# A graph layer's attention row: made by transposing the features' last column and kept in PSUM, in place of a product with a repeated weight

## The chip, the cores and the metric

The kernel runs on one core of one Trainium2 chip. The metric is the device time of one execution in microseconds; the value quoted for a kernel is the median of several executions. Beside them stands one execution taken by the hardware profiler, from which all the durations come.

## The reference

32 entries of 512 nodes with 256 features pass through four layers. Layers 0 and 3 score pairs of nodes and need the score only where the adjacency matrix is not zero. Layer 1 is a residual graph convolution. Layer 2 is the one that matters here (cut, without its batch sizes):

```python
feats = jnp.einsum('bni,oi->bno', data, W1)
f1 = jnp.einsum('bno,o->bn', feats, W2) + b2[0]
logits = f1[:, :, None] + f1[:, None, :]
coefs = jax.nn.softmax(jax.nn.leaky_relu(logits) + bias1, axis=-1)
vals = jnp.einsum('bij,bjo->bio', coefs, feats)
return vals + bias2 + data
```

So each entry has a number f1 per node, and the logits need it twice: as a column (one number per row of the matrix) and as a row (the same 512 numbers on all the partitions). `bias1` is the adjacency matrix.

## The kernel before, in words

All the numbers are fp32. The adjacency matrix is sparse, so a sparse path runs (`Sparse`, `sparse_path`); a dense path stands in the program too and isn't taken with this input. The 32 entries go in eight groups of four; group 0 has the entries 0 to 3, and the entries of a group are called b0 to b3 here.

Five kinds of work exist for each group, written as generators that yield after each piece:

- `first` (L717): loads an entry, transposes it to `hT`, writes it back as `xT`, and multiplies it by the first weights (`pre`, L540), which fills a table in DRAM that the edges read.
- `edges` (L586): the sparse scores, once for layer 0 and once for layer 3. For 36 items a group, GpSimd (POOL) fetches rows of the table by an indirect DMA (L582), DVE adds (L654, 128x1024), and four DVE steps (L667, 128x256) reduce them; POOL then puts the scores into cells in DRAM by an indirect DMA (L576), from where `load` (L689) reads them back.
- `middle` (L750, `middle_one` L787): the rest of layer 0, and the layers 1 and 2, entry by entry. This is the "main" stream.
- `last` (L960, with `sums` L933): the rest of layer 3.
- the preparations of the start.

`weave` (L443) merges them by due times. The main stream's pieces have shares (`middle_shares`, L992) that spread them over a group. Where a piece of the main stream yields True, one or two pieces of the "fill" kind (`first` and `last`) are put behind it, to give TensorE work while the main stream waits. What `weave` makes is a program order; a scheduler of the framework then orders each engine's instructions, so that DVE's queue mixes edge steps, filling steps and the main stream[...]. Group 0 has no filling pieces in `middle`, and the last group's are few.

In `middle_one`, the part around the change: `yT` is completed by a DVE add (L829). Then `f1` is a product of a repeated weight vector `q_bc` with `yT` (L834), two matmuls of 128x512 that give the row on all 128 partitions at once, copied from PSUM to SBUF by ACT (L835). The weight vector is W1 times W2, computed at the start and stored as the last column of `WT_2` (L164) and repeated into `q_bc` (L165). For each of the four blocks of rows, two matmuls of 128x257 (L845) give the features and, in column 256, f1 as a column; ACT copies the features (L846); DVE adds twice the bias to the column (L849); ACT adds row and column (L851); DVE makes the leaky relu (L852), adds the adjacency and takes the smallest negated value (L854); ACT takes the exponent with its sum (L855); DVE inverts and scales (L856, L857). `put_back` (L891) transposes the block on TensorE (L896) and copies it into `eT` (L897). When all four blocks are there, `feats` times `eT` follows (L873), and the DVE step L874 ends the layer.

PSUM results of all these come from one pool of 8 buffers of one bank each (L437).

Of the kernel before, what the change touches and what calls it, by code (L numbers as in the profile page):

```python
# [8 lines left out]
F32 = mybir.dt.float32  # L9
BF16 = mybir.dt.bfloat16  # L10
I32 = mybir.dt.int32
AF = mybir.ActivationFunctionType
ALU = mybir.AluOpType
AX = mybir.AxisListType
PSUM = bass.MemoryType.PSUM

P = 128
N = 512
D = 256
NC = N // P  # L20
DC = D // P
# [18 lines left out]
def mm(nc, out, pairs):  # L40

    for n, (lhsT, rhs) in enumerate(pairs):
        nc.tensor.matmul(out, lhsT, rhs, start=(n == 0), stop=(n == len(pairs) - 1))  # L43


class Model:


    def __init__(self, ctx, tc, a):
        nc = self.nc = tc.nc  # L50
        self.tc, self.a = tc, a
        const = self.const = ctx.enter_context(tc.tile_pool(name="const", bufs=1))
        self.ident = const.tile([P, P], F32, name="ident")
        make_identity(nc, self.ident)
        self.adj = const.tile([P, NC, N], F32, name="adj")
        for c in range(NC):
            nc.sync.dma_start(self.adj[:, c, :], a["adj"][c * P : (c + 1) * P, :])
        self.g0, self.g3 = self.gnn_first("L0_gnn"), self.gnn_first("L3_gnn")
# [78 lines left out]
    def others_loads(self, raw):  # L137
        nc, a, const = self.nc, self.a, self.const
        self.b_1 = self.column("L1_gnn_b")
        self.w2 = self.column("L2_gnn_W2")  # L140
        self.b2 = self.bcast("L2_gnn_b2", 1)
        self.bias2 = self.column("L2_gnn_bias2")
        self.W1_1, self.W1_2 = raw([P, DC, D]), raw([P, DC, D])
        nc.scalar.dma_start(self.W1_1, a["L1_gnn_W"].rearrange("(c p) d -> p c d", p=P))
        nc.scalar.dma_start(self.W1_2, a["L2_gnn_W1"].rearrange("(c p) i -> p c i", p=P))
        self.twob2 = const.tile([P, 1], F32, name="twob2")
        self.WT_1 = const.tile([P, DC, D], F32, name="WT_1")
        self.WT_2 = const.tile([P, DC, D + 1], F32, name="WT_2")
        self.q_bc = const.tile([P, DC, P], F32, name="q_bc")

    def others(self, psum):
        nc = self.nc
        nc.vector.tensor_scalar(self.twob2, self.b2, 2.0, None, ALU.mult)
        for src, dst in ((self.W1_1, self.WT_1), (self.W1_2, self.WT_2)):
            for c in range(DC):
                pt = psum()
                for r in range(DC):
                    nc.tensor.transpose(pt[:, r * P : (r + 1) * P], src[:, r, c * P : (c + 1) * P], self.ident)
                nc.vector.tensor_copy(dst[:, c, 0:D], pt[:, 0:D])
            yield  # L160
        for c in range(DC):
            pq = psum()[:, 0:1]
            mm(nc, pq, [(self.W1_2[:, r, c * P : (c + 1) * P], self.w2[:, r, :]) for r in range(DC)])
            nc.vector.tensor_copy(self.WT_2[:, c, D : D + 1], pq)  # L164
            nc.vector.tensor_copy(self.q_bc[:, c, :], self.WT_2[:, c, D : D + 1].to_broadcast([P, P]))  # L165
        yield

    def adj_turned(self, c, psum):
# [246 lines left out]
class Sparse:  # L415
# [3 lines left out]
    def __init__(self, ctx, m, counts, xr, outr, B):  # L419
        self.m, self.nc, self.tc, self.counts = m, m.nc, m.tc, counts  # L420
        tc = m.tc
        self.xr, self.outr = xr, outr
        pool = lambda n, b, **k: ctx.enter_context(tc.tile_pool(name=n, bufs=b, **k))
        self.dram = pool("dram", 1, space=bass.MemoryType.DRAM)

        self.cells = {
            k: [self.dram.tile([CELLS + SPARE, NB], F32, name=f"cells_{k}{q}") for q in range(2)] for k in "03"
        }
        self.lists = self.dram.tile([N, 2 * N], F32, name="lists")
        self.x2s = self.dram.tile([B, P, NC, D], F32, name="x2s")  # L430

        self.xT, self.x2T = (self.dram.tile([B, P, DC, N], F32, name=n) for n in ("xT", "x2T"))
        self.e = Edges(m, pool("edges", 1))
        self.adjT = pool("adjT1", 1).tile([P, NC, N], F32, name="adjT")
        self.grp = pool("grp", 2)
        self.act, self.small, self.gath = pool("act", 1), pool("small", 2), pool("gath", 5)
        self.ps = pool("ps", 8, space=PSUM)  # L437
        self.later, self.bigs, self.given = None, 0, None

    def psum(self):  # L440
        return self.ps.tile([P, N], F32, name="pst", tag="pst")
# [345 lines left out]
    def middle_one(self, g0, g3, b, i, SA, keep, given):  # L787
        nc, m, w = self.nc, self.m, g0.w
        act, small, psum = self.act, self.small, self.psum
# [34 lines left out]
        yT = act.tile([P, DC, N], F32, name="yT")  # L824
# [4 lines left out]
            nc.vector.tensor_tensor(yT[:, c, :], yT[:, c, :], zT[:, c, :], ALU.add)  # L829
            yield c == DC - 1  # L830

        f1 = small.tile([P, N], F32, name="f1", bufs=1)
        pf = psum()
        mm(nc, pf, [(m.q_bc[:, c, :], yT[:, c, :]) for c in range(DC)])  # L834
        nc.scalar.copy(f1, pf)  # L835
        feats = act.tile([P, NC, D], F32, name="feats", tag="mhT0")
        eT = act.tile([P, NC, N], F32, name="eT")
        if more:
            keep[1] = turned()
            ahead = None if given else self.hWa(g0, keep[1], 0)  # L840
        yield
        exs = []
        for ic in range(NC):
            pn = psum()
            mm(nc, pn[:, 0 : D + 1], [(yT[:, r, ic * P : (ic + 1) * P], m.WT_2[:, r, :]) for r in range(DC)])  # L845
            nc.scalar.copy(feats[:, ic, :], pn[:, 0:D])  # L846
            cols = small.tile([P, 4], F32, name="cols", bufs=4)
            fcol, mn, total, rs = (cols[:, k : k + 1] for k in range(4))
            nc.vector.tensor_scalar(fcol, pn[:, D : D + 1], m.twob2, None, ALU.add)  # L849
            ex = small.tile([P, N], F32, name="ex", bufs=4)  # L850
            nc.scalar.activation(ex, f1, AF.Identity, bias=fcol)  # L851
            nc.vector.scalar_tensor_tensor(ex, ex, 0.01, ex, ALU.mult, ALU.max)  # L852

            nc.vector.tensor_tensor_reduce(ex, ex, m.adj[:, ic, :], -1.0, 3.0e38, ALU.add, ALU.min, mn)  # L854
            nc.scalar.activation(ex, ex, AF.Exp, bias=mn, scale=-1.0, accum_out=total)  # L855
            nc.vector.reciprocal(rs, total)  # L856
            nc.vector.tensor_scalar(ex, ex, rs, None, ALU.mult)  # L857
            exs.append(ex)
            yield True
            if ic > 1:  # L860
                self.put_back(eT, ic - 2, exs[ic - 2])
                yield True
# [129 lines left out]
def middle_shares(given):  # L992


    hWa = [] if given else [1.7, 1.7]
    shares = list(hWa)
    for b in range(NB):
        more = hWa if b < NB - 1 else []
        shares += [] if given else [2.8, 2.8]
        shares += [3.4, 3.4, 1.0, 2.7]  # L1000
        shares += [1.7, 3.4, 2.8, 4.5, 1.7]
        shares += [0.4, 0.4, 0.4, 1.0, 0.4, 1.0] + more + [1.5, 1.5]
        shares += [2.8, 4.5] + [0.4] * NC + [0.5, 0.5]
    return shares + [0.1]
# [46 lines left out]
def dense_path(ctx, m, xr, outr, B):  # L1051

    nc, tc, a = m.nc, m.tc, m.a
    keep = ctx.enter_context(tc.tile_pool(name="keep", bufs=1))
    act = ctx.enter_context(tc.tile_pool(name="dact", bufs=1))
    hidp = ctx.enter_context(tc.tile_pool(name="hid", bufs=4))
    small = ctx.enter_context(tc.tile_pool(name="dsmall", bufs=2))
    ps_s = ctx.enter_context(tc.tile_pool(name="ps_s", bufs=2, space=PSUM))
    ps = ctx.enter_context(tc.tile_pool(name="dps", bufs=5, space=PSUM))

    def psum(n=N):
        t = ps.tile([P, N], F32, name="dpst", tag="dpst")
        return t[:, 0:n]

    ones_row = keep.tile([1, P], F32, name="ones_row")
    nc.vector.memset(ones_row, 1.0)
    for _ in m.rest(keep.tile([P, 2048], F32, name="raw"), psum):
        pass
    adjT = keep.tile([P, NC, N], F32, name="adjT")
    for c in range(NC):  # L1070
        nc.scalar.copy(adjT[:, c, :], m.adj_turned(c, psum))
# [111 lines left out]
    def layer2(y):  # L1183
        yT = transposed(y, "dyT")
        f1 = act.tile([P, N], F32, name="df1")
        pf = psum()
        mm(nc, pf, [(m.q_bc[:, c, :], yT[:, c, :]) for c in range(DC)])
        nc.scalar.copy(f1, pf)
        feats = act.tile([P, NC, D + 1], F32, name="dfeats")
        fcol = act.tile([P, NC, 1], F32, name="dfcol")  # L1190
        yb = act.tile([P, NC, D], F32, name="dyb")
        nc.gpsimd.memset(feats[:, :, D : D + 1], 1.0)
        for c in range(NC):
            pn = psum(D + 1)
# [5 lines left out]
        for ic in range(NC):  # L1200
# [9 lines left out]
            ex = small.tile([P, N], F32, name="dex")  # L1210
# [9 lines left out]
            rs = small.tile([P, 1], F32, name="drs")  # L1220
# [61 lines left out]
```

## Time and profile before

| what | value |
|---|---|
| median of 3 executions | 3247.94 us (3246.24 to 3251.05) |
| the profiled execution | 3230.9 us |
| its span, first to last instruction | 3229.2 us |
| mean granted TensorE clock | 0.928 |
| L43, the product with `q_bc` | 128 records, 62.3 us busy |
| L835, the copy of f1 | 32, 18.8 us busy |
| L849, the column's bias | 128, 26.7 us busy |
| L896, the transposes of `ex` | 512, 88.5 us busy, 99.2 us idle before them |

A matmul in fp32 shows as two records of TensorE (PE), and a transpose as one. Ends of matmuls are modelled, so the time that one takes is best read from its start to the next start. DVE steps overlap a little at their ends as well: their mean durations add up to some 5 to 7% more than the time that a run of them takes. "PEclk" is the share of the clock that was granted. In the lists a bracket such as `[1.05 <-DVE ex L857]` says that the engine stood idle for 1.05 us and which instruction released it.

### The profile page before, as it was taken

To read this page: it belongs to the slowest core of one execution; us is meant where nothing else is said; L and a number is where in the kernel's file an instruction comes from. 1 tells how busy PE (TensorE), PEld (TensorE's weight loads), DVE (VectorE), ACT (ScalarE), POOL (GpSimd) and SP (SyncE) were. 2 spreads that over 40 slices of the span, in tenths; PEclk is the share of its full clock that TensorE was granted. 3 is DMA by queue.
4 is the path that set the end of the run, shared out by engine and by line. 5 is a ranking of instruction groups with operands and counts; after the bars stand their busy time and mean duration, and the time that the engine had idled before them with its cause. 6 is when DMAs were issued, how large, how long until landed. Compare 5 with 4: busy or idle time off the path is not lost.

```text
span 3229.2 us, 32451 instructions
## 1 busy us (share of the span) xinstructions
PE 2773.2 (86%) x8646; PEld 1656.2 (51%) x8646; DVE 2371.6 (73%) x7692; ACT 1007.0 (31%) x2341; POOL 1488.3 (46%) x1248
## 2 busy tenths in 40 slices
PE   6346887989997999979999899979998899999947
PEld 3223444546554566435654565536654465545626
DVE  7777736989596976969598786969688695953662
ACT  4452333322233222333223232333223222232441
POOL 1565402747264543636354462636355362630371
PEclk9677898999999999989999999989999999999969
DMA  8876425777567766776577766776577765640663
GB/s 273 295 246 229 152 91 166 261 262 224 188 226 240 234 196 202 249 241 220 173 230 235 245 203 211 237 250 207 178 219 246 242 221 190 219 159 33 209 201 112
DMA packets 302718, 679.40 MB, mean 210 GB/s; under 512 B 52672, under 2 KB 170944, under 8 KB 294336
## 3 DMA queue, kind: packets, MB, share of 16 engines
q0 software_dynamic: 111168, 338.90, 32.8%
q1 hardware_dynamic: 186224, 334.68, 31.0%
q10 hardware_dynamic: 5136, 3.68, 0.4%
q8 instruction: 71, 1.16, 0.1%
q14 instruction: 119, 0.97, 0.1%
HBM read 531.12 MB, written 146.01 MB: 210 GB/s over the span
## 4 chain that ended last, share of the span: by engine, by line
PE 38%; DVE 34%; DMA 17%; issue 6%; ACT 3%; POOL 1%; SPq 0%; ACTq 0%; POOLq 0%; DVEq 0%
PE pst L43 28%; DVE rows L667 11%; DVE rows L654 10%; DMA rows<-table,iv 6%; DMA table<-puv 4%; PE pst L945 4%; PE pst L802 2%; DMA cells<-s,cell 2%; PE pst L954 1%; DVE ex L852 1%; PE pst L896 1%; DMA cells<-self_s 1%; PE pst L809 1%; DVE ex L854 1%; DMA mine<-table,iu 1%
## 5 line engine op out<-in xcount | busy, mean ns | idle before, releaser
L582 POOL DMA_INDIRECT rows<-table,iv x554 | 680.1, 1228 | 1047.4 <-DMA table<-puv 383.1
L576 POOL DMA_INDIRECT cells<-s,cell x576 | 684.3, 1188 | 592.7 <-DMA cells<-s,cell 357.0
L654 DVE TENSOR_TENSOR rows<-rows,mine 128x1024 f32<-128x1024 f32 x554 | 667.3, 1215 | 195.0 <-DMA rows<-table,iv 178.9
L667 DVE SCALAR_TENSOR_TENSOR rows<-rows,L_gnn_W2bc 128x256 f32<-128x256 f32 x2016 | 750.9, 413 | 0.4
L43 PE MATMUL pst<-adj,h 128*128 128x512 f32 x1024 | 453.5, 592 | 0.0
L43 PE MATMUL pst<-L_gnn_Wa,hT 128*128 128x256 f32 x1024 | 260.6, 408 | 142.4 <-DMA hT<-xT 69.4
L43 PE MATMUL pst<-w_L_gnn_W,hT 128*128 128x512 f32 x512 | 261.2, 646 | 57.4 <-ACT hT L537 46.3
L43 PEld LDWEIGHTS pst<-adj,h 128*128 128x128 f32 x1024 | 192.8, 190 | 219.5 <-issue 214.1
L43 PEld LDWEIGHTS pst<-L_gnn_Wa,hT 128*128 128x128 f32 x1024 | 207.8, 208 | 187.8 <-issue 103.2
L43 PE MATMUL pst<-w_L_gnn_W,yT 128*128 128x512 f32 x512 | 239.9, 622 | 66.0 <-DVE yT L874 66.0
L43 PE MATMUL pst<-eT,feats 128*128 128x512 f32 x512 | 240.0, 624 | 9.1 <-ACT eT L897 9.1
L43 PE MATMUL pst<-adjT,zW 128*128 128x512 f32 x512 | 225.9, 592 | 0.0
L550 ACT COPY puv<-pst 128x256 f32<-128x256 f32 x256 | 94.7, 372 | 412.5 <-DVE puv L549 376.2
L945 PEld LDWEIGHTS pst<-hWa,SA 128*128 128x128 f32 x896 | 213.4, 328 | 5.9 <-issue 3.3
L945 PE MATMUL pst<-hWa,SA 128*128 128x256 f32 x896 | 216.2, 397 | 0.0
L43 PEld LDWEIGHTS pst<-w_L_gnn_W,yT 128*128 128x128 f32 x512 | 101.8, 200 | 196.3 <-issue 111.0
L549 DVE TENSOR_TENSOR puv<-pst,bc_L_gnn_b 128x256 f32<-128x256 f32 x256 | 106.6, 417 | 127.4 <-PE pst L43 64.4
L771 ACT COPY flat<-SA 128x512 f32<-128x512 f32 x128 | 134.5, 1122 | 203.3 <-PE pst L43 178.8
L802 PE MATMUL pst<-flat,hWa 128*128 128x512 f32 x448 | 196.8, 592 | 0.0
L43 PEld LDWEIGHTS pst<-w_L_gnn_W,hT 128*128 128x128 f32 x512 | 102.0, 206 | 168.0 <-issue 90.5
L43 PE MATMUL pst<-WT,hT 128*128 128x256 f32 x512 | 141.8, 434 | 38.8 <-DVE hT L810 38.8
L896 PE MATMUL pst<-ident,ex 128*128 128x128 f32 x512 | 88.5, 302 | 99.2 <-DVE ex L857 62.6
(167 smaller groups left out, 3728.0 us busy)
## 6 DMA issues: line engine op xcount, KB each, us to landing
table<-puv SPq DMA_DIRECT2D x256, 256.0 KB, 4.9
SA<-cells SPq DMA_DIRECT2D x64, 1024.0 KB, 7.0
h<-in_x_dram SPq DMA_DIRECT2D x64, 512.0 KB, 6.6
mine<-table SPq DMA_DIRECT2D x64, 512.0 KB, 6.2
hT<-xT SPq DMA_DIRECT2D x36, 512.0 KB, 5.0
h<-x2s SPq DMA_DIRECT2D x36, 512.0 KB, 6.1
xT<-hT SPq DMA_DIRECT2D x32, 512.0 KB, 7.5
x2T<-yT SPq DMA_DIRECT2D x32, 512.0 KB, 5.0
```

The source lines that it names most:

```text
L43: nc.tensor.matmul(out, lhsT, rhs, start=(n == 0), stop=(n == len(pairs) - 1))
L549: nc.vector.tensor_tensor(puv[:, 0, :], pp[:, 0:D], w["b1bc"], ALU.add)
L550: nc.scalar.copy(puv[:, 1, :], pp[:, D:])
L576: self.nc.gpsimd.indirect_dma_start(out=g.cells[half], out_offset=bass.IndirectOffsetOnAxis(ap=at, axis=0), in_=s, in_offset=None)
L582: self.nc.gpsimd.indirect_dma_start(out=rows, out_offset=None, in_=g.table, in_offset=bass.IndirectOffsetOnAxis(ap=at, axis=0))
L654: nc.vector.tensor_tensor(rows, rows, other, ALU.add)
L667: nc.vector.scalar_tensor_tensor(part, part, 0.0, w["W2bc"], ALU.max, ALU.mult, accum_out=at)
L771: self.nc.scalar.copy(flat[:, r, :], SA[r][:, :, b])
L802: nc.tensor.matmul(pz, hWa[:, r, cs], flat[:, r, :], start=(r == 0), stop=False)
L809: nc.tensor.matmul(pz, w["Wm"][:, d, cs], mhT[:, d, :], start=False, stop=(d == DC - 1))
L896: nc.tensor.transpose(pt[:, js], ex[:, js], self.m.ident)
L945: nc.tensor.matmul(pz[:, k * D : (k + 1) * D], SA[r][:, cs, b], hWa[:, r, :], start=(r + k == 0), stop=False)
```

## The change

The product with `q_bc` goes, and so does its copy to SBUF. All four blocks' features are made first, 257 columns wide, so that f1's column lies in SBUF with them. One DVE step adds twice the bias to all four columns. Four transposes on TensorE, each of a column repeated 128 times, write the row onto all the partitions of a PSUM bank, and ACT's step reads the row from there. The bank is a pool of its own; the common pool has 7 buffers. The features yield four pieces, of which the third and fourth allow filling work, and no feature matmuls stand between the softmax blocks. `q_bc` is kept for the dense path alone.

```diff
-        self.ps = pool("ps", 8, space=PSUM)
+        self.ps = pool("ps", 7, space=PSUM)
+        self.ps_f1 = pool("ps_f1", 1, space=PSUM)
...
-        f1 = small.tile([P, N], F32, name="f1", bufs=1)
-        pf = psum()
-        mm(nc, pf, [(m.q_bc[:, c, :], yT[:, c, :]) for c in range(DC)])
-        nc.scalar.copy(f1, pf)
-        feats = act.tile([P, NC, D], F32, name="feats", tag="mhT0")
+        feats = act.tile([P, NC, D + 1], F32, name="feats", tag="mhT0")
         eT = act.tile([P, NC, N], F32, name="eT")
         if more:
             keep[1] = turned()
             ahead = None if given else self.hWa(g0, keep[1], 0)
-        yield
-        exs = []
         for ic in range(NC):
             pn = psum()
             mm(nc, pn[:, 0 : D + 1], [(yT[:, r, ic * P : (ic + 1) * P], m.WT_2[:, r, :]) for r in range(DC)])
-            nc.scalar.copy(feats[:, ic, :], pn[:, 0:D])
+            nc.scalar.copy(feats[:, ic, :], pn[:, 0 : D + 1])
+            yield ic > 1
+
+        fcol = small.tile([P, NC, 1], F32, name="fcol", bufs=1)
+        nc.vector.tensor_scalar(fcol, feats[:, :, D : D + 1], m.twob2, None, ALU.add)
+        f1 = self.ps_f1.tile([P, N], F32, name="f1")
+        for ic in range(NC):
+            nc.tensor.transpose(
+                f1[:, ic * P : (ic + 1) * P], feats[:, ic, D : D + 1].to_broadcast([P, P]), m.ident
+            )
+        exs = []
+        for ic in range(NC):
             cols = small.tile([P, 4], F32, name="cols", bufs=4)
-            fcol, mn, total, rs = (cols[:, k : k + 1] for k in range(4))
-            nc.vector.tensor_scalar(fcol, pn[:, D : D + 1], m.twob2, None, ALU.add)
+            mn, total, rs = (cols[:, k : k + 1] for k in range(3))
             ex = small.tile([P, N], F32, name="ex", bufs=4)
-            nc.scalar.activation(ex, f1, AF.Identity, bias=fcol)
+            nc.scalar.activation(ex, f1, AF.Identity, bias=fcol[:, ic, :])
...
-        shares += [1.7, 3.4, 2.8, 4.5, 1.7]
+        shares += [1.7, 3.4, 2.8, 4.5] + [0.9] * NC
```

In the changed kernel the lines of the sparse path move: the features' copy is L839, the columns' bias L843, the new transposes L846, row plus column L854, and the four steps after it L855, L857, L858 and L859 with L860; the edge steps L654 and L667 are L653 and L666 there, L712, L938 and L957 are L711, L941 and L960, and L874 is L877.

More of the change, by code (lines that the diff above doesn't have):

```diff
@@ L148, in others_loads @@
         self.WT_2 = const.tile([P, DC, D + 1], F32, name="WT_2")
-        self.q_bc = const.tile([P, DC, P], F32, name="q_bc")
     def others(self, psum):
@@ L164, in others @@
             nc.vector.tensor_copy(self.WT_2[:, c, D : D + 1], pq)
-            nc.vector.tensor_copy(self.q_bc[:, c, :], self.WT_2[:, c, D : D + 1].to_broadcast([P, P]))
         yield
@@ L1063, in psum @@
         return t[:, 0:n]
+    q_bc = keep.tile([P, DC, P], F32, name="q_bc")
     ones_row = keep.tile([1, P], F32, name="ones_row")
@@ L1068, in dense_path @@
         pass
+    for c in range(DC):
+        nc.vector.tensor_copy(q_bc[:, c, :], m.WT_2[:, c, D : D + 1].to_broadcast([P, P]))
     adjT = keep.tile([P, NC, N], F32, name="adjT")
@@ L1186, in layer2 @@
         pf = psum()
-        mm(nc, pf, [(m.q_bc[:, c, :], yT[:, c, :]) for c in range(DC)])
+        mm(nc, pf, [(q_bc[:, c, :], yT[:, c, :]) for c in range(DC)])
         nc.scalar.copy(f1, pf)
```

## The prediction

> **What bounds the kernel now.** I read the page first, then the PE's waits, then a table of stretches, then the timelines of one softmax stage on PE and on DVE.
>
> ```profile
> span 3229.2 us, 32451 instructions
> ...
> PE 2773.2 (86%) x8646; PEld 1656.2 (51%) x8646; DVE 2371.6 (73%) x7692; ACT 1007.0 (31%) x2341; POOL 1488.3 (46%) x1248
> ...
> PE 38%; DVE 34%; DMA 17%; issue 6%; ACT 3%; POOL 1%; SPq 0%; ACTq 0%; POOLq 0%; DVEq 0%
> ```
>
> PE and DVE share the chain that ended last, so no single engine's busy time is the bound. The next view has a row for each stretch from the f1 product to the first product with `eT`: entries b0, b1, b2, b3 of group 2, then an entry of group 0, which has no filling work.
>
> ```profile
> core 0: us, PE busy (x) PEld busy (x) DVE busy (x) ACT busy (x) POOL busy (x), PEclk, DMA share, GB/s
> 909.90:936.10 26.20, 22.73 (x109) 19.46 (x108) 26.20 (x89) 11.42 (x25) 17.98 (x15) 1.00 0.50 152
> 995.90:1033.40 37.50, 30.36 (x101) 17.63 (x99) 25.00 (x92) 16.85 (x40) 10.16 (x10) 0.86 0.58 202
> 1101.10:1128.80 27.70, 25.10 (x117) 21.74 (x116) 27.64 (x96) 12.01 (x26) 21.00 (x18) 1.00 0.74 239
> 1188.70:1211.80 23.10, 22.63 (x92) 16.29 (x90) 12.05 (x29) 11.30 (x23) 2.72 (x3) 1.00 0.64 216
> 419.70:438.00 18.30, 9.84 (x37) 6.71 (x35) 9.23 (x25) 11.72 (x24) 0.00 (x0) 0.83 0.08 30
> ```
>
> In b0 and b2 DVE never rests; in b3 PE never does; b1 waits; in group 0 both rest and the chain of dependent steps sets the time. b2 in detail, on PE and then on DVE:
>
> ```profile
> 1101.09 1.88 PE L43 MATMUL pst<-yT,q_bc 128*128 128x512 f32 x4
> 1102.80 1.03 PE L43 MATMUL pst<-WT,yT 128*128 128x257 f32 x4
> 1103.67 7.63 PE L945 MATMUL pst<-hWa,SA 128*128 128x256 f32 x32
> ...
> 1116.33 0.60 PE L896 MATMUL pst<-ident,ex 128*128 128x128 f32 x4
> ...
> 1118.85 0.63 PE L896 MATMUL pst<-ident,ex 128*128 128x128 f32 x4 [1.05 <-DVE ex L857]
> ...
> 1128.84 0.59 PE L43 MATMUL pst<-eT,feats 128*128 128x512 f32 x1
> ```
>
> ```profile
> 1099.57 0.68 DVE L829 TENSOR_TENSOR yT<-yT,hT 128x512 f32<-128x512 f32 x1
> ...
> 1110.20 0.48 DVE L857 TENSOR_SCALAR ex<-ex,cols 128x512 f32<-128x512 f32 x1
> ```
>
> PE fills the time until the first `ex` (ready at 1110.7) with feats and with the last layer's products, and waits only 1.05 and 1.55 us for later ones.
>
> [...]four 128x128 transposes take 0.44 us to the next start (1116.33 to 1116.77), while four matmul records of 128x512, which are two matmuls, take 1.71 (1101.09 to 1102.80). [...] Here a gap of 1.95 us was enough:
>
> ```profile
> 1298.00 3.04 PE L43 MATMUL pst<-L_gnn_Wa,hT 128*128 128x256 f32 x8
> ...
> 1298.60:1302.00 3.40, 3.40 (x11) 2.72 (x11) 3.40 (x17) 2.16 (x6) 2.63 (x3) 0.50 0.70 157
> ```
>
> The same eight took 1.89 at full clock (1119.31). [...]
>
> **The change, part by part** (against the profiled execution: 3230.9 us, of which 3229.2 span; it lies 17.0 under the median of 3247.94, and I shift my sum by that).
>
> *Removed.* Two products per entry: 1.71 us of PE, 32 entries. The f1 copy on ACT (L835, 0.59) lies beside PE's feats and is worth nothing except where the chain is bare. Three of four L849 (0.13 to the next start each): 0.4 us of DVE an entry. Two setup copies of q_bc, 0.4 us once.
>
> *Added.* Four transposes: 0.44 us of PE, if a repeated column loads like `ex`. The trace has no such load; a bound above is the 328 ns weight load of L945 against 155 for L896, +0.7 an entry, below it is nothing less than 0.44. I take 0.44, so PE gains 1.27 an entry, 41 us in all. L851 reading PSUM: 685 ns (L828, from PSUM) against 718, nothing. 257 columns in feats' copy: nothing.
>
> *Moved: the softmax start.* All four feats, the whole fcol and the transposes now come before the first exponent; before, the first exponent needed one feats. Then the four chains run abreast. No DMA's work is changed; SP passes the same descriptors, with hT's read one table write earlier, and the SA load still ahead of the xT write that b1 waits for (SP issues it at 1009.21, xT at 1009.63).
>
> *Group 0 and the tail (no filling work).* Entry at 419.75: its last L829 ends 421.36. New chain: feats copied 423.8, transposes 424.1, four L854 of 0.63 to 427.0, DVE's second and third steps interleaved (eight of 0.6, with Exp of 0.9 beside), first `ex` 430.7, last 433.3, transposes and copy (at half clock) 435.2. Before, eT was complete at 438.02: gain 2.8. The old order had the last chain start only at 432.4, after its feats had waited behind a transpose; that wait disappears and next late is DVE itself. Entries 0 and 1 have DVE edge steps between: the sum of DVE work before the fourth `ex` falls from 18.9 and 19.9 to 13.4 and 13.0, gain 5 and 6. Likewise entry 4: 2.6; 29: 4; 30: 2.1; 31: 2.3; entry 28 loses 0.6. Together about -27 us.
>
> *b2 (six entries).* In the built order DVE has before the first L860: 22 L666 of 0.345, 6 L653 of 1.215, 10 steps of 128x512 at 0.68, the multiply 0.49 and 0.7 of small ones and accumulator reads; 22.9 us by rows. The old order's sum to the first L874 is 34.6 by rows and took 32.8, so I scale by 0.945: 21.6, and `ex` is ready at 1100.25 + 21.6 = 1121.9. PE wants it at 1101.1 + six feats matmuls 2.6 + filling 3.7 + 0.9 + 3.7 + transposes 0.44 + 3.6 = 1116.0. It waits 5.9. The second `ex` costs 0.75, the third 1.0, and filling 1.8 + 3.6 + 1.8 follows: the eT product starts at 1132.5 instead of 1128.8, and 0.8 later still for a part of a half-clock window: +4.5. What is queued behind: `h` and eT products, and all of PE. The old sum to the first `ex` was 11.1. This is the main loss.
>
> *b0 (five entries).* The same with 25.3 by rows times 0.934 (37.0 took 34.55): 23.65 after the L829 that ends at 905.46. PE starts feats 4.6 later and wants `ex` at 19.5: waits 4.1, 0.8, 0.8, and reaches the eT product 31.7 after 905.46 instead of 30.7: +1.0.
>
> *b3 (six).* No edges. The transposes wait for 3.6 and 3.4 us of filling work; first `ex` 5.4 us after them, PE wants it after 3.4: waits 2.0 and 0.9 less 1.27 gained, less the old 0.5: +0.4, and 0.5 us of filling goes elsewhere: +1.
>
> *b1 (six).* PE's time hangs on the xT write (7.4 us from 1009.63) and on the filling pieces after it; it gains about what lies after: -1.
>
> *Bunched edges.* In b0 and b2 DVE now asks for six edge steps in 17 to 20 us. POOL needs a fetch (1.23) and a put (1.19) for each with 0.30 between, 3.0 us; DVE asks each 2.8 to 3.2. With three fetched ahead it is nearly enough: bounds 0 and 3, I take 1.0 for eleven entries: +11.
>
> Sum: -27 + 27 + 5 + 6 - 6 + 11 = +16: 3246.9 profiled, 3264 as a median.
>
> **Rivals.**
> *A, faster.* The edge steps pulled forward (one more in b0's stretch, two in b2's, about 2.7 us each) are DVE work that later need not be done. PE waits per group for edges' ends: 1.8 and 4.6 in b1, 12.45 for yT behind the next edges' first row, 3 for zT at 1255. If the SA load is released as much earlier as the edges are, b0 and b2 are repaid: about 32 of the loss goes, without the POOL stretch too: -27, 3221. Against it: the 12.45 hangs on the new table's landing, not on old edges. It decides from 3 us per group given back.
> *B, seven banks.* PE waits for a bank that DVE holds (L960 and L711 stand behind edges). The trace has no PE wait of that kind; at 1 us an entry, +32 more: 3296.
> *C, a wash.* The PE gain of 41 and the waits cancel: 3248.
> That the product stays is excluded: the built order has no q_bc in the sparse path.
>
> **How the numbers follow.** Forecast (slower, 3255 to 3285) 0.45; A 0.25; C 0.20; B and worse 0.10. This kernel's times can tell about 0.2%, 6.5 us, from no change. Faster 0.25, same 0.20, slower 0.55. The range 3222 to 3300 leaves out part of A and of B; the likeliest case's own is 3255 to 3285.
>
> **What would show it.** Right: the idle before the `ex` transposes (99.2 us in the groups by line now) grows to about 150 while group 0's shrinks; q_bc's 62 us of PE are gone and 14 of transposes appear; the edge rows (L653) wait longer for POOL. Wrong: PE waits of under 2 us in b2, or PE waiting for evacuation steps, or L854's mean well above 0.72.

## The result, and the profile after

The changed kernel takes 3224.22 us (median of 11 executions, 3217.82 to 3237.16); the kernel before, beside it on the same chip, 3247.25 us (11 executions). The ratio is 0.9939 with a 95% interval of 0.9928 to 0.995: 0.6% faster. On a second chip it was 0.9953 (0.994 to 0.9966). The forecast was slower, 3264. The page of the changed kernel, in the lines that answer to those of before:

```profile
span 3220.7 us, 32267 instructions
...
PE 2741.7 (85%) x8645; PEld 1652.4 (51%) x8646; DVE 2351.1 (73%) x7594; ACT 980.4 (30%) x2309; POOL 1472.2 (46%) x1248
...
PE 35%; DVE 27%; DMA 12%; issue 5%; ACT 2%; POOL 1%; SPq 0%; DVEq 0%; ACTq 0%; POOLq 0%
```

PE's busy time fell by 31.5 us against the first profile, the span by 8.5 only, and the medians by 23. The first profile of before was a quick execution, or one on a quicker chip: at 3230.9 us it lies under all eleven executions timed beside the change (3238.42 to 3251.05), its chip isn't known, and three of the chips used below have medians of 3229 to 3231 for this kernel. A second profile of the same kernel (the run "again" below) has a span of 3251.9, and I compare with that one from here on. Cut at two marks in every entry, the DVE add that completes `yT` ("y") and the first product with `eT`, the two traces differ like this, in us, entries 0 to 31:

| stretch | predicted | measured, after less again |
|---|---|---|
| group 0, y to eT, four entries | -16.6 | -19.1 |
| entry 4 and the tail (28 to 31), y to eT | -10.4 | -7.0 |
| b2, y to eT, one entry (mean of groups 2 to 6) | +4.5 | +4.15 |
| b0 | +1.0 | +2.5 |
| b1 | -1 | +3.7 |
| b3 | +1 | 0.0 |
| from eT to the next y: ahead of b0, b1, b2, b3 | 0, and +1 for POOL | 0.0, -2.6, -6.3, 0.0 |
| groups 1 to 6 without entry 4's own stretch, sum | +43 | +7 |

So the gains of group 0 came, and the later `eT` products of the steady groups came too, even more of them than forecast. But what lies between the stretches grew shorter by 9 us a group, and that the forecast had not. The next two views show it for b1 and b2 of group 2: four stretches each (from eT of b0 to y of b1, from y to eT of b1, from eT of b1 to y of b2, from y to eT of b2), first of before (the run again), then of after.

```profile
core 0: us, PE busy (x) PEld busy (x) DVE busy (x) ACT busy (x) POOL busy (x), PEclk, DMA share, GB/s
948.02:1007.60 59.58, 57.99 (x156) 27.71 (x154) 55.97 (x207) 16.07 (x31) 38.90 (x34) 1.00 0.83 272
1007.60:1045.08 37.48, 29.70 (x99) 17.48 (x98) 24.93 (x91) 16.85 (x40) 10.89 (x10) 0.86 0.63 203
1045.08:1110.45 65.37, 54.44 (x145) 27.51 (x146) 47.71 (x162) 12.90 (x22) 27.92 (x22) 0.92 0.79 246
1110.45:1141.58 31.13, 27.69 (x118) 23.65 (x117) 28.80 (x98) 11.97 (x26) 21.32 (x19) 0.89 0.72 232
```

```profile
core 0: us, PE busy (x) PEld busy (x) DVE busy (x) ACT busy (x) POOL busy (x), PEclk, DMA share, GB/s
922.62:979.00 56.38, 55.76 (x152) 27.09 (x150) 54.63 (x203) 15.72 (x30) 36.29 (x31) 1.00 0.83 268
979.00:1020.95 41.95, 28.95 (x104) 17.08 (x103) 25.55 (x92) 16.49 (x40) 11.99 (x11) 0.88 0.70 235
1020.95:1081.11 60.16, 51.78 (x135) 26.12 (x136) 44.65 (x152) 12.87 (x22) 24.92 (x20) 0.91 0.75 227
1081.11:1115.51 34.40, 30.15 (x126) 24.98 (x125) 32.69 (x106) 11.38 (x25) 23.88 (x21) 0.90 0.70 226
```

The first column after the window is its length: +4.47 in b1 and +3.27 in b2, and -3.20 and -5.21 ahead of them. The PE counts tell half of the reason: ahead of b2 there are 135 matmul records where there were 145, and in b2 there are 126 where there were 118 (four of the product are gone, and four transposes are in). Filling work went over. The timelines of PE show which; before (again), then after:

```profile
1096.56 3.60 PE L43 MATMUL pst<-adj,h 128*128 128x512 f32 x8
1099.99 7.03 PE L43 MATMUL pst<-adjT,zW 128*128 128x512 f32 x16
1106.86 3.60 PE L43 MATMUL pst<-adj,h 128*128 128x512 f32 x8
1110.29 1.88 PE L43 MATMUL pst<-yT,q_bc 128*128 128x512 f32 x4
...
1130.44 0.88 PE L896 MATMUL pst<-ident,ex 128*128 128x128 f32 x3 [3.44 <-DVE ex L857]
```

```profile
1077.84 0.59 PE L43 MATMUL pst<-adjT,zW 128*128 128x512 f32 x1
1078.27 7.03 PE L43 MATMUL pst<-adj,h 128*128 128x512 f32 x16
1085.13 2.77 PE L43 MATMUL pst<-WT,yT 128*128 128x257 f32 x12
...
1096.08 0.60 PE L846 MATMUL f<-ident,feats 128*128 128x128 f32 x4
1096.51 3.62 PE L957 MATMUL pst<-L_gnn_Wm,mhT 128*128 128x256 f32 x16
1104.38 2.17 PE L899 MATMUL pst<-ident,ex 128*128 128x128 f32 x8 [4.25 <-DVE ex L860]
...
1115.51 1.02 PE L43 MATMUL pst<-eT,feats 128*128 128x512 f32 x2
```

Before, eight records of `adj,h` (filling work) stood ahead of the products that make `yT` (`adjT,zW`) and eight behind; after, all 16 stand behind, so 4.0 us of filling lie between y (at 1081.11) and the features. Averaged over the groups 2 to 6, b2's stretch holds 3.8 us more of `adj,h` and the stretch ahead of it 3.8 us less. The new transposes take 0.43 us to the next start, close to the forecast's 0.44, and the wait for the first exponential is there, 4.25 us. The groups by line, with the idle time ahead of them in the third field, again and then after:

```profile
L896 PE MATMUL pst<-ident,ex 128*128 128x128 f32 x512 | 90.3, 306 | 108.3 <-DVE ex L857 75.8 <-DVE cols L856 19.6 <-DVE s L571 5.9
L43 PE MATMUL pst<-w_L_gnn_W,yT 128*128 128x512 f32 x512 | 237.0, 616 | 72.9 <-DVE yT L874 72.9
L654 DVE TENSOR_TENSOR rows<-rows,mine 128x1024 f32<-128x1024 f32 x554 | 667.9, 1216 | 206.7 <-DMA rows<-table,iv 189.6 <-DMA mine<-table,iu 16.9
```

```profile
L899 PE MATMUL pst<-ident,ex 128*128 128x128 f32 x512 | 97.1, 329 | 105.7 <-DVE ex L860 59.5 <-DVE cols L859 45.9
L43 PE MATMUL pst<-w_L_gnn_W,yT 128*128 128x512 f32 x512 | 240.5, 623 | 44.9 <-DVE yT L877 44.9
L653 DVE TENSOR_TENSOR rows<-rows,mine 128x1024 f32<-128x1024 f32 x554 | 667.6, 1217 | 185.5 <-DMA rows<-table,iv 158.0 <-DMA mine<-table,iu 27.3
L846 PE MATMUL f<-ident,feats 128*128 128x128 f32 x128 | 21.9, 277 | 0.8
```

The waits for `ex` are not 150 us but 106, the wait for `yT` at the end of b1 fell from 73 to 45, and the edge rows wait less, not more.

For the steady groups I use one account more. A group's length is PE's idle time (the length less PE's busy time), plus the clock that was not granted while PE was busy (half of the busy time at half clock; half clock while PE idles is in the idle time already), plus the rest, which is PE's work at full clock. Means of the groups 2 to 6 from one profiled execution of each kernel; the experiments are told below:

| kernel | one group, us | PE idle | clock lost | work |
|---|---|---|---|---|
| before: first profile, again | 370.7, 372.7 | 31.4, 33.9 | 10.0, 9.5 | 329.4, 329.3 |
| after: first profile, after2 | 374.1, 374.6 | 37.0, 37.8 | 12.8, 12.4 | 324.3, 324.4 |
| ordprod | 382.2 | 37.7 | 15.0 | 329.5 |
| f1sbuf | 380.5 | 39.7 | 16.7 | 324.1 |
| shares17 | 377.6 | 40.0 | 13.2 | 324.4 |
| noprod | 369.4 | 34.9 | 11.2 | 323.3 |
| early, early2 | 366.6, 368.5 | 32.2, 32.7 | 9.3, 10.9 | 325.1, 324.9 |
| earlyprod | 368.5 | 29.4 | 9.9 | 329.2 |
| pad1 | 376.2 | 36.2 | 12.1 | 327.8 |
| pad3 | 377.4 | 35.1 | 14.3 | 328.0 |

After against again: work -4.9, idle +3.1, clock lost +3.3, so +1.5 a group. The work is about 329 us in every kernel with the product and 324 to 325 with the transposes (pad1 and pad3 add 3.4 to that), so the product's time is really saved; in the steady groups waits and half clock eat it up. From chip to chip the median of the kernel before goes from 3229 to 3252 us, which would be 2.6 us in a group. A smaller difference between rows from different chips, the +1.5 among them, is therefore not shown by this table; that the groups 1 to 7 together come out even is shown by the run steadynew.

### The profile page after: what moved, and what is told of

It is laid out like the page before. It is cut to its first block, busy times and chain, and to the rows that moved or that the text cites. A ratio compares the mean times of both kernels' runs of the same rounds, so it can differ in the third digit from the quotient of the medians.

```text
span 3220.7 us, 32267 instructions
## 1 busy us (share of the span) xinstructions
PE 2741.7 (85%) x8645; PEld 1652.4 (51%) x8646; DVE 2351.1 (73%) x7594; ACT 980.4 (30%) x2309; POOL 1472.2 (46%) x1248
## 3 DMA queue, kind: packets, MB, share of 16 engines
q0 software_dynamic: 111168, 338.90, 33.9%
## 4 chain that ended last, share of the span: by engine, by line
PE 35%; DVE 27%; DMA 12%; issue 5%; ACT 2%; POOL 1%; SPq 0%; DVEq 0%; ACTq 0%; POOLq 0%
PE pst L43 24%; DVE rows L666 9%; DVE rows L653 8%; DMA rows<-table,iv 5%; PE pst L948 4%; DMA table<-puv 3%; PE pst L801 2%; DMA cells<-s,cell 2%; PE pst L899 2%; PE pst L957 1%; DVE ex L855 1%; DMA mine<-table,iu 1%; PE pst L808 1%; DVE both L551 1%; DVE puv L548 1%
## 5 line engine op out<-in xcount | busy, mean ns | idle before, releaser
L581 POOL DMA_INDIRECT rows<-table,iv x554 | 671.2, 1212 | 1060.3 <-DMA table<-puv 392.8
L653 DVE TENSOR_TENSOR rows<-rows,mine 128x1024 f32<-128x1024 f32 x554 | 667.6, 1217 | 185.5 <-DMA rows<-table,iv 158.0
L666 DVE SCALAR_TENSOR_TENSOR rows<-rows,L_gnn_W2bc 128x256 f32<-128x256 f32 x2016 | 749.4, 416 | 0.4
L43 PE MATMUL pst<-L_gnn_Wa,hT 128*128 128x256 f32 x1024 | 274.1, 423 | 131.6 <-DMA hT<-xT 75.9
L43 PEld LDWEIGHTS pst<-L_gnn_Wa,hT 128*128 128x128 f32 x1024 | 216.5, 217 | 176.4 <-issue 104.6
L948 PE MATMUL pst<-hWa,SA 128*128 128x256 f32 x896 | 217.2, 398 | 0.0
L948 PEld LDWEIGHTS pst<-hWa,SA 128*128 128x128 f32 x896 | 213.8, 328 | 6.0 <-issue 3.3
L899 PE MATMUL pst<-ident,ex 128*128 128x128 f32 x512 | 97.1, 329 | 105.7 <-DVE ex L860 59.5
L566 ACT ACTIVATE s<-s,L_gnn_nb 128x16 f32<-128x16 f32 (+2 forms) x176 | 53.5, 304 | 411.4 <-DVE rows L666 399.6
```

The lines of the kernel that those rows point to most:

```text
L566: self.nc.scalar.activation(t, t, AF.Exp, bias=w["nb2"], scale=-1.0)
L581: self.nc.gpsimd.indirect_dma_start(out=rows, out_offset=None, in_=g.table, in_offset=bass.IndirectOffsetOnAxis(ap=at, axis=0))
L653: nc.vector.tensor_tensor(rows, rows, other, ALU.add)
L666: nc.vector.scalar_tensor_tensor(part, part, 0.0, w["W2bc"], ALU.max, ALU.mult, accum_out=at)
L899: nc.tensor.transpose(pt[:, js], ex[:, js], self.m.ident)
L948: nc.tensor.matmul(pz[:, k * D : (k + 1) * D], SA[r][:, cs, b], hWa[:, r, :], start=(r + k == 0), stop=False)
```

## The experiments

My theory on seeing the result: the new order makes group 0 and the tail shorter, and in the steady groups it costs about what the transposes save. The rivals: the saved PE time makes the gain everywhere; or it is the seven banks or the first profile that misled. All ratios are to the kernel before on the same chip. The kernels of one set ran on one chip. The sets were: again, bank7, ordprod and g0new; steadynew, shares17, noprod and early; f1sbuf, earlyprod and earlysh; pad1 and pad3; after2 and early2.

**again**: the kernel before, no edit.

> The kernel before, unchanged, profiled once more. The profiled execution of before took 3230.9 us where its executions have a median of 3247; that of after took 3222.5, at its own median of 3224. If the first profile of before was only a lucky one, this profile lies near 3247 and the 16 us between the two profiles lie in the steady groups 1 to 6, where the profile of after shows 20 us more than the first profile of before. If instead the steady groups of before take the same time here as in its first profile, the gain of 23 us is somewhere that I have not seen. The ratio of the times is 1.000.

Ratio 1.0 (0.9988 to 1.0013); span of the profile 3251.9. Up to the last entry's first product with `eT` it is 20.9 us behind the first profile, and nearly all of that lies in b2's stretches (+10.5 from y to eT, +8.2 ahead of it, six entries). So the steady groups of the first profile were the quick ones, and b2's old waits of 1.05 and 1.55 us, with which I forecast, are short: b2 waits 3.6 us as a mean here, 3.0 there.

**bank7**:

```diff
-        self.ps = pool("ps", 8, space=PSUM)
+        self.ps = pool("ps", 7, space=PSUM)
```

> The kernel before with a common PSUM pool of 7 buffers in place of 8, and nothing else. My theory (the softmax order brings the gain in group 0 and the tail, and the steady groups come out even): no change, 3247 within 6 us, because PE nowhere waits for a bank in the trace of before. The rival (seven banks cost time, and the change gains more than it shows): 1 us an entry or more, 3265 to 3280, and gaps of PE released by copies of older results.

Ratio 1.0006 (0.9996 to 1.0017). Rival B of the forecast falls: in the old order a bank less cost nothing.

**ordprod**:

```diff
         f1 = self.ps_f1.tile([P, N], F32, name="f1")
-        for ic in range(NC):
-            nc.tensor.transpose(
-                f1[:, ic * P : (ic + 1) * P], feats[:, ic, D : D + 1].to_broadcast([P, P]), m.ident
-            )
+        mm(nc, f1, [(m.q_bc[:, c, :], yT[:, c, :]) for c in range(DC)])
```

(Not shown: `q_bc` is made at the start again.)

> The changed kernel in everything but one thing: the row f1 is again the product of the repeated weight with yT (two matmuls of 128x512), written into f1's own bank at the place of the four transposes. So the order, the shares and the banks of after with the PE work of before: 1.27 us of PE an entry more than after. If the order makes the gain: group 0 and the tail keep it less 1.27 an entry (8 entries, 10 us), and in the steady groups the waits of PE for the first exponential (4.2 us in b0 and b2, 1.6 in b3) and for hT (10 in b1) take the 1.27 in: 3224 + 10 = 3234, within 5. If the PE time makes it: 32 times 1.27, 41 us, 3265.

3292.25 us, ratio 1.0132 (1.0113 to 1.0151). Both expectations fall: the same order with the product is 1.3% slower than before, and 1.8 to 1.9% slower than with the transposes, 60 us for 41 us of PE. Group 0 and the tail pay 17 us (10 expected); of the 19.1 us that group 0 gains from y to eT, this run keeps 11.2, so the order alone makes more than half of it. In the steady groups the waits did not take the 1.27 us in, for a reason that I had overlooked: the product stands ahead of the chain, so the first exponents end 0.9 to 1.3 us later, and PE's wait behind it stays (b2 4.7 us in both). With it the order alone costs 9.5 us in each steady group (382.2 against 372.7 on the same chip: idle time +3.8, clock lost +5.5), which is what I had forecast in kind; the transposes give 8.1 back, of which 5.2 are work and 2.3 clock.

**g0new**: both ways stand in the kernel, and a flag chooses; `given` is set in group 0 alone.

```diff
+        new = bool(given)
+        if not new:
...
+            mm(nc, pf, [(m.q_bc[:, c, :], yT[:, c, :]) for c in range(DC)])
...
-        shares += [1.7, 3.4, 2.8, 4.5] + [0.9] * NC
+        shares += [1.7, 3.4, 2.8, 4.5] + ([0.9] * NC if given else [1.7])
```

> The changed way in group 0 alone (features first, transposes, f1 in PSUM, its shares), the old way (product, interleaved softmax, its shares) in the groups 1 to 7; banks 7 and 1. The profiles of after and before differ by -19.7 us at the end of group 0's last softmax. If group 0 and the tail make the gain and the steady groups come out even: 3247 - 20 = 3227, within 5. If the gain is spread over all entries as PE time: 4 of 32 entries' part of 23, 3 us, 3244.

3228.75, ratio 0.9941 (0.9922 to 0.9959): 19 us. Group 0's four stretches shorten by 19.2 us, as in after. Entry 2 of group 0 after, its stretch and PE in it:

```profile
410.80:423.80 13.00, 6.52 (x30) 5.12 (x28) 7.21 (x21) 10.50 (x22) 0.00 (x0) 0.74 0.12 42
```

```profile
412.68 0.95 PE L846 MATMUL f<-ident,feats 128*128 128x128 f32 x4
419.33 3.80 PE L899 MATMUL pst<-ident,ex 128*128 128x128 f32 x16 [5.70 <-DVE cols L859]
423.81 1.55 PE L43 MATMUL pst<-eT,feats 128*128 128x512 f32 x3 [0.67 <-ACT eT L900]
```

It takes 13.0 us from y, where the forecast had 13.8 and before took 16.7: the four chains run abreast and one long wait is left.

**steadynew**: the complement.

```diff
-        new = bool(given)
+        new = not given
...
-        shares += [1.7, 3.4, 2.8, 4.5] + ([0.9] * NC if given else [1.7])
+        shares += [1.7, 3.4, 2.8, 4.5] + ([0.9] * NC if not given else [1.7])
```

> The complement of the run that changed group 0 alone: group 0 the old way, groups 1 to 7 the changed way with its shares. If the parts add up (group 0 alone gave -23 us by medians, -20 by the ratio; all together -23): -3 to -6, 3246, with the last group giving 6 and the steady groups costing 2. If group 0's new way is also what lets the later groups start well: slower than before, 3255 or more.

3239.78, ratio 1.0009 (0.9998 to 1.002). The parts add up: -0.59% and +0.09%, where both together gave -0.61% and -0.47%. Group 0 is the whole net gain: by the first table, the rest of the groups 1 to 6 loses what entry 4 and the tail gain (+7 and -7.0).

**shares17**:

```diff
-        shares += [1.7, 3.4, 2.8, 4.5] + [0.9] * NC
+        shares += [1.7, 3.4, 2.8, 4.5] + [0.425] * NC
```

> The changed kernel with the features' four pieces at 0.425 each, 1.7 together as the one piece before, instead of 3.6; so the edges' due times stand against the main stream as before. Built, b2 has 5 edge steps instead of 6 ahead of the first exponential, b0 has 6 still. Theory one (edge steps pulled forward are repaid, rival A of the prediction): no gain, 3224 within 6; b2's wait falls by 1 to 3 us and the yT wait (9.0 us in after, 12.4 before) grows by as much. If edge steps pulled forward are the loss that the prediction counted: 3 us in each b2 stay won, 3224 - 18 = 3206.

3244.95, ratio 1.0029 (1.0017 to 1.0041), 0.8 to 0.9% slower than after: neither number. A group is 3.4 us longer than in after, and b3 alone 3.6, where a filling piece moved behind three blocks' transposes (waits of 1.55, 0.41 and 1.77 us in a row, a PEclk of 0.62 from 1192.67 to 1200.62, and 5.88 us for the 16 records of L948 behind them, where after took 4.00). The other three entries cancel to 0.2: b2 3.0 shorter from y to eT and 2.2 longer ahead of it, b1 1.4 longer in all. So in this profile edge steps pulled forward are repaid, and b2's wait did not even fall (5.5).

**noprod**: the product goes from the kernel before, with its copy; a part of the adjacency matrix stands in for the row, so what comes out is not the layer's result.

```diff
-        f1 = small.tile([P, N], F32, name="f1", bufs=1)
-        pf = psum()
-        mm(nc, pf, [(m.q_bc[:, c, :], yT[:, c, :]) for c in range(DC)])
-        nc.scalar.copy(f1, pf)
+        f1 = m.adj[:, 0, :]
```

> The kernel before without the product and its copy: the row f1 is replaced by the first 128 rows of the adjacency matrix, so the logits are other numbers and the exponents need not wait for a product. 1.71 us of PE an entry fall away in the old order. Theory one (PE time counts in the steady groups: there after's order cost 8.1 us a group more with the product than with the transposes, for 5.1 us of PE): -2 to -2.7 an entry in 24 steady entries, and in group 0 and the tail the 1.71 and a copy of 0.6 on the bare chain, -18: 3250 - 48 to -65 - 18 = 3167 to 3184. Theory two (the edges' chain sets the steady groups' length, and the old order's waits take the PE time in): -18 and 1.7 in each b3, 3222.

3200.06, ratio 0.9889 (0.987 to 0.9907), 36 us for 55 us of PE: between the two. In the old order a steady group gains 3.3 us against again for the 6.8 of four products: the work falls by 6.0, and idle time takes 1.0 and the clock 1.7 of it. This split is rough, since again ran on another chip and the profiled execution was the slowest of noprod's four.

**f1sbuf**: in after, ACT copies the row to SBUF.

```diff
+        f1 = small.tile([P, N], F32, name="f1", bufs=1)
+        nc.scalar.copy(f1, pf)
```

(Not shown: `pf` is the bank that the transposes write.)

> The changed kernel with one copy more: the row of f1 is copied by ACT from its PSUM bank to SBUF, as before, and ACT's step reads it there. If keeping it in PSUM matters where the chain is bare: +0.6 to 0.9 us in each entry of group 0 and the tail (+6), and in the steady groups +0.6 in b0, b2 and b3 of which half comes back (+6): 0.4% over after, a ratio to the kernel before of 0.998. If ACT (30% busy) hides the copy: the ratio of after, 0.994.

3264.6, ratio 1.0103 (1.0086 to 1.012), far over both expectations: 1.5 to 1.7% over after, 50 us, for a copy of 0.6 us in 32 entries. A group is 6.3 longer: 2.7 of idle time and 3.9 of clock. (The built order moves with it: 7 edge steps instead of 6 stand ahead of b0's first exponential.) b3 shows how a short delay is doubled; after, then f1sbuf:

```profile
1191.32 0.66 PE L899 MATMUL pst<-ident,ex 128*128 128x128 f32 x4 [1.55 <-DVE ex L860]
1192.39 0.66 PE L899 MATMUL pst<-ident,ex 128*128 128x128 f32 x4 [0.41 <-DVE ex L860]
1192.88 4.00 PE L948 MATMUL pst<-hWa,SA 128*128 128x256 f32 x16
```

```profile
1199.33 0.66 PE L901 MATMUL pst<-ident,ex 128*128 128x128 f32 x4 [2.27 <-DVE ex L862]
1200.99 0.66 PE L901 MATMUL pst<-ident,ex 128*128 128x128 f32 x4 [1.00 <-DVE ex L862]
1201.49 5.51 PE L950 MATMUL pst<-hWa,SA 128*128 128x256 f32 x16
```

The two waits grow by 0.72 and 0.59, and then the same 16 records take 5.51 us instead of 4.00: PEclk is 0.79 in the 8 us from 1199.30, where it is 1.00 in those from 1191.30 in after. It is 0.79 behind these waits in three of the five b3 and 1.00 in two.

**early**: the filling work behind the transposes instead of ahead of them.

```diff
-            yield ic > 1
+            if ic < NC - 1:
+                yield False
...
                 f1[:, ic * P : (ic + 1) * P], feats[:, ic, D : D + 1].to_broadcast([P, P]), m.ident
             )
+        yield True
```

> The changed kernel with its filling work moved: none between the features and the transposes of f1, and the piece that yields True stands right behind the transposes. In the built order DVE then has 2 edge steps instead of 6 before the first exponential in b2 and 3 instead of 6 in b0, and PE has 10 us of filling between the transposes and the first exponential's transposes. Theory one (the order costs about 9 us of a steady group because edge steps and filling stand ahead of the chain, and the transposes' PE time pays it back): PE's waits for the first exponential (4.6 us in b0, 4.7 in b2, 2.0 in b3, means of after) fall under 1 us each, 9 us a group; half of it comes back as longer waits in b1 for hT and in b2 for yT, so -5 a group: 3224 - 30 = 3194, within 15. Theory two (the steady groups' length is set by the edges, the cells' load and hT, whatever PE does): only b3's 2 us are won, 3212, and the waits in b1 and for yT grow by 7 us a group.

3175.71, ratio 0.9825 (0.9805 to 0.9845), about 39 us under after, where the theories had 30 (within 15) and 12; beside after on one chip (**early2** with **after2**) 3171.99 against 3214.6. It beats both kernels. The stretches from y to eT of b0 and b3 in group 2 of after (b2's stands above), and those of b0, b2 and b3 here:

```profile
889.47:922.62 33.15, 28.27 (x122) 22.69 (x120) 31.19 (x102) 11.08 (x25) 21.64 (x19) 0.95 0.60 181
...
1175.25:1198.48 23.23, 21.27 (x90) 15.56 (x88) 10.42 (x27) 10.27 (x22) 2.78 (x3) 1.00 0.59 200
```

```profile
882.89:909.56 26.67, 24.51 (x116) 20.62 (x114) 26.67 (x90) 10.43 (x25) 15.76 (x13) 1.00 0.56 169
...
1076.53:1105.03 28.50, 27.20 (x125) 23.06 (x124) 28.50 (x101) 11.22 (x25) 21.14 (x18) 1.00 0.63 200
...
1164.78:1185.60 20.82, 20.82 (x90) 15.57 (x89) 10.57 (x26) 9.96 (x22) 4.50 (x4) 1.00 0.47 145
```

33.2, 34.4 and 23.2 us in after became 26.7, 28.5 and 20.8, with a PEclk of 1.00. By the means of the groups 2 to 6 the three win 15.1 us, of which the stretches ahead of b1 and b2 give back 2.2 and 7.0; a group ends 7.5 us shorter (idle -4.8, clock -3.4, work +0.7), and 6.1 shorter in early2 against after2, on one chip.

> The early order, unchanged, in one set with the changed kernel: if the ratios hold between sets, 0.9825 within 0.2% and 1.15% under the changed kernel.

> The changed kernel unchanged, beside the kernel before on one more chip, and in one set with the early order. The kernel before took 3231 to 3252 us in the sets so far, so times of different sets are compared by their ratios to it. If that is sound, the ratio is again 0.994 within 0.2%. If it moves by more (0.997 or 0.991), the prices of single edits that I have taken from ratios of different sets are uncertain by 10 us.

early2 0.9822 (0.9802 to 0.9843), after2 0.9953: ratios of different sets agree within 0.15%, 5 us.

**earlyprod**: early with the product.

```diff
-        for ic in range(NC):
-            nc.tensor.transpose(f1[:, ic * P : (ic + 1) * P], feats[:, ic, D : D + 1].to_broadcast([P, P]), m.ident)
+        mm(nc, f1, [(m.q_bc[:, c, :], yT[:, c, :]) for c in range(DC)])
         yield True
```

> The early order (features, row of f1, filling behind it) with the product of the repeated weight in place of the four transposes: 1.27 us of PE an entry more than the run with the early order. Theory one (PE's time by the records is all that the transposes save): +41 us, 1.3%, a ratio to the kernel before of 0.995; the order alone is then worth 0.5% without any transpose. Theory two (the product costs what it cost in the order of after, 66 us or 2.1 an entry, since it also lengthens waits and half-clock stretches): 1.003.

3194.92, ratio 0.9903 (0.9876 to 0.9929). The order alone, without any transpose, gains 1%; and here the transposes are worth 0.8%, 25 us by the ratios (20 by the medians beside earlysh, on one chip), less than both theories. The work differs by 4.1 us a group from early, and idle time takes 2.8 of it.

**earlysh**: early with the shares of shares17.

```diff
-        shares += [1.7, 3.4, 2.8, 4.5] + [0.9] * NC
+        shares += [1.7, 3.4, 2.8, 4.5] + [0.425] * NC
```

> The early order with the features' pieces at 0.425 each instead of 0.9, so that the edges' due times stand against the main stream as in the kernel before. In after the same edit made it 0.9% slower; its profile puts that on b3 alone (21.5 us in six entries, where a filling piece moved behind three blocks' transposes), with the other entries' gains and losses cancelling. If b3's filling was the cause: in the early order b3 has no waits to lengthen (10 us of filling stand ahead), so the same time as the early order, 0.9825 within 0.3%. If edge steps that come earlier against the main stream are a gain in themselves: 0.9% slower here too, 0.991.

3175.32, ratio 0.9827 (0.981 to 0.9844): as early. With b3's 3.6 us in shares17, this fits that b3's filling made shares17 slow, and not the edges.

**pad1** and **pad3**: eight matmuls of the features once more, in b1 or in b3.

```diff
+        if b == 1 and not given:
+            for ic in range(NC):
+                pn = psum()
+                mm(nc, pn[:, 0 : D + 1], [(yT[:, r, ic * P : (ic + 1) * P], m.WT_2[:, r, :]) for r in range(DC)])
         xT = yT
```

> The changed kernel with 3.44 us of PE work added in b1 of the groups 1 to 7: the features' eight matmuls are made a second time, right ahead of the first product with eT, into buffers that nobody reads. Theory (PE's wait for yT at the end of b1, 9.0 us, ends at a fixed time, about 147 us after the yT of b0 is complete, when the first edge row of the next set can be added; what b0 and b1 lose ahead of it is taken in there): the six steady groups pay 0 to 1 us each and the last group 3.4, together 3 to 9, a ratio to the kernel before of 0.995 to 0.997, and the wait for yT falls to about 5.6. Rival (a loss of PE time anywhere in a steady group lengthens it): 7 times 3.44, 24 us, 1.001.

> The same addition in b3 of the groups 1 to 7, where PE never rests and no wait follows until b0's hT of the next entry: both theories expect the whole 7 times 3.44, 24 us, a ratio of 1.001; if less than 15, the gates reach into b3 too.

pad1 3232.49, ratio 1.0003 (0.9986 to 1.0019); pad3 3247.34, ratio 1.0052 (1.0037 to 1.0067). On one chip the same 3.44 us cost 15 us less in b1 than in b3, 2.1 in each of seven groups. By the profiles a steady group grows by 2.0 in pad1 and by 3.3 in pad3. So the waits behind b1 do take in a part, but not nearly all, as my theory had it: the wait for `yT` fell from 9.0 to 7.5 only, and b2's wait for its first exponential rose from 4.7 to 6.2.

## Why the prediction was wrong

- **Group 0 and the tail: right.** -27 forecast, -26 measured in the stretches from y to eT (-19.1 and -7.0); g0new shows 19 us for group 0 by itself.
- **The single prices: right.** Transposes 0.44 (0.43 measured; a matmul of as many columns takes 0.86, half of the product's 1.71, so column for column the traces show a factor of two), a repeated column loads like `ex` (weight load 137 ns in the median, 142 for `ex`), the step from PSUM 687 ns (685 forecast), the features' copy 374 ns with 257 columns (370 with 256), seven banks nothing (a ratio of 1.0006 in the old order).
- **b2, "This is the main loss", +4.5 in each of six entries: the failed step.** The first exponential came 23.5 us after y (21.6 forecast) and eT 34.8 after it (32.3 forecast, and 0.8 for half clock). So the delay of eT was there, +4.15 by the mean for +4.5. The fault was to book a later eT as lost time, and to put at nothing what the stretch ahead of it would give back: that one became 6.3 us shorter, so the two together end 2.15 us earlier. From y to eT 3.8 us are filling work that the stretch ahead of y no longer has, which I had not seen in the built order: I let PE start the features 0.85 us after y, where 4.0 passed. So PE asked in group 2 for the first exponential 3.3 us later than I had it, DVE had it ready 1.6 us later (it waits 1.35 us for edge rows there), and 5.9 became 4.25; and ahead of y 3.8 us are given back. The wait for `yT` there is also 3.5 shorter. In the group's account PE's idle time grew by 3.1 us, where my waits came to 9.7 more than before (2.2 in b0, 5.1 in b2, 2.4 in b3). By stretch: b0 +1.0, b2 +1.1, b3 +1.5, b1 +3.5, mostly for hT, and -3.5 ahead of b2, for yT. A part of the rest is the first profile, whose b2 waited less (3.0 us against 3.6).
- **b0, b3, b1.** First exponential of b0 after 23.9 us (23.65 forecast), its waits 4.2, 0.4 and 0.3 in group 2 (4.1, 0.8, 0.8), b3's 1.55 and 0.41 (2.0 and 0.9): right to half a microsecond. b0's eT still came 1.5 us later than forecast; a PEclk of 0.95 in its stretch of group 2 (1.00 in again) makes 1.7. b1 was called -1 and came +3.7, with 2.6 back ahead of it.
- **Half clock: too small.** 0.8 in b2 forecast, 3.3 a group measured.
- **Bunched edges, +11: wrong.** The edge rows waited 21 us less in all than in again (9.5 less than in the first profile). From y to eT they wait in b2's stretch alone, 1.7 us, where it was 1.5 in again already.
- **Rival A had the number, 3221, and not the whole mechanism.** That what is pulled forward is repaid fits shares17 and earlysh. But of the load of the cells, which was to come earlier, the first part is issued at the same time, 103 us after b0's y in both kernels (102.8 to 104.2 and 101.3 to 105.3 in the groups 2 to 6), and the second too; the third and fourth parts come 3 and 9 us earlier, but in these groups no engine's wait ends on any of them. Filling work that changes places and the shorter wait for yT repay.
- **PE's 41 us have no fixed price.** The same saving is worth about 60 us in after's order and 20 to 25 in the early one. Against that, the steady groups' even result is a cancelling of two large terms: order +57 (six times 9.5) and transposes -49 (six times 8.1), where I had +73 and -30.

pad1 and pad3 cost 18 and 34 us by the ratios (against the mean of after's two, 0.9946), and their profiled executions lie only 12 and 20 us above after2's. Most of that gap is a matter of which execution was profiled: after2's lies 6.1 us over the median of its set, and pad3's, the quickest of its twelve, 6.7 us under.

What stays open: why b1's wait for hT grew by 3.2 us, and how much of the shorter wait for `yT` comes from edge steps pulled forward and how much from the longer stretches before it. The second has a part: in pad1, 3.44 us of work more before the wait cut it by 1.5.

## What to carry to other kernels

A stretch that ends later is a loss only after its neighbours have been read: list the filling work in it and ahead of it, and the wait that follows, and add over the whole period. Steps that start a long chain on other engines (here the features and the row of f1) belong ahead of the filling work, not behind it. Here the edge steps ahead of the first exponential fell with it from six to three in b0 and to two in b2, and with the same instructions it was worth 1.3%. Before a forecast of under 1%, take a second profile of the kernel before, and compare profiles of one chip: the two differed by 0.7%.

## What the runs showed of the hardware

Half clock came the more often, the longer PE's gap was. In all 17 traces, from 890 to 2760 us, PE gaps that stood alone (none over 0.3 us in the 8 us before and 5 us after) were followed by half clock in 0 of 164 cases from 0.3 to 1.5 us, in 5 of 30 from 1.5 to 2 (three of them in the first profile of before, the 1.95 us ahead of 1297.53 that the prediction names among them), in 20 of 33 from 2 to 2.5, in 13 of 17 from 2.5 to 3, and in all of 91 from 3 to 6. The half clock lasted 3.41 us after 73 of these 129 gaps and 6.83 us after the other 56. In b3 of f1sbuf, above, 0.7 us more on a chain cost twice that again in clock: a wait grew from 1.55 to 2.27 us, and the 16 records behind it took 1.51 us longer.
